# Two layers of attention and feed-forward: small VectorE steps moved to ScalarE and GpSimd, ternary weights taken later

## The chip, the cores and the metric

The kernel runs on one core of a Trainium2 chip. The metric is the device time of one execution in microseconds (us). The kernel before was timed in three runs: 1294.21, 1289.97 and 1292.45 us, median 1292.45. One more execution was profiled; times of single instructions come from it. PE is TensorE, DVE is VectorE, ACT is ScalarE, POOL is GpSimd, SP is the engine that issues most DMAs. "L842" is line 842 of the kernel before.

## What is computed

Two transformer layers over x of 2 batches, 1024 tokens, 256 features. In each, attention and feed-forward read the same normalised x and are both added to x.

```python
xn = layernorm(x)
x = x + attn0(xn) + ffn0(xn)     # attn0: 32 query heads of 8, 8 key heads, causal, rope, biases
xn = layernorm(x)
x = x + attn1(xn) + ffn1(xn)     # attn1: at each token, its 16 heads attend to each other
# ffn0: fp8 (e4m3) products: (gelu(x8 @ g0) * (x8 @ g1)) rounded to fp8, @ w_linear
# ffn1: silu(gate) * up, rms_norm, @ w_proj; both weights made ternary in groups of 64
```

## The kernel before, in words

**Layer 0** is one function, `attention0`. Its queries are cut into 16 tiles of 128 (batch 0 tiles 0 to 7, then batch 1 tiles 7 down to 0). A tile needs two passes over the scores. The first (`max_unit`) makes them on PE in pairs of PSUM banks from a pool of three (`ps_s`), and VectorE reduces each bank to row maxima (L842). `take_max` splits the maxima of a tile into three bf16 parts, `turn_max` transposes them on PE, copies them out of PSUM on VectorE (L867) and sends them through DRAM into the rows of `qlast`. The second pass (`weigh`) makes the scores again, transposed and with the maximum already subtracted by these rows, in banks of `ps_t` (four), and ScalarE takes the exponential (L906); `gather` multiplies by v (L914); `normalise` transposes and divides; `turn_rows` transposes again and copies out of PSUM on VectorE (L947); `output` multiplies by wo, and VectorE adds the product to x (L955).

PE's order is the program's order. The program is written in slots: one slot is a part of the second pass of the tile that is due, plus as many first-pass units of later tiles as a credit allows (`one_slot`, `advance`), at most three tiles ahead, plus one piece of the feed-forward. `after(n, f)` puts f some slots later. A tile's second pass begins ten slots after its maxima are complete (`LEAD`). The other engines take their instructions in an order that a scheduler chose when the program was built, each engine strictly in that order, so one that waits holds up all behind it.

**Feed-forward 0** (`ffn0`) runs in these slots, in 16 pieces of 256 hidden features (four token blocks, four pieces each). Per piece, ScalarE casts the gate and up products to bf16 (L284); VectorE does gelu's polynomial in five steps on 128x1024 bf16 (L287 to L291), ScalarE the tanh (L292), VectorE three more steps (L294 to L296), and `e4m3` rounds to fp8 (L180 to L185). With `check`, `e4m3` adds two steps that turn values beyond fp8's range into NaN (L188, L189). `weights0` rounds the six weight blocks in the same way at the start. `out_piece` makes the result of 128 tokens; ScalarE casts it to bf16 (L250), POOL adds it and a bias to x (L252, L253).

**Ternary weights** for layer 1 are made during layer 0, in 12 pieces (eight of w_gate_up, four of w_proj; `ternary`). Each is loaded from POOL's queue (L317); then one VectorE step (L320), a group sum on PE (L323), three VectorE steps (L325, L327, L328) and four POOL steps (L329 to L332), the last of which writes the bf16 result. The next piece's L320 overwrites a buffer that these POOL steps read. One piece is taken each time a tile's maxima are complete (`next_weights` in `advance`), so with the first twelve tiles. At the end `wgu_bf` is cast to fp32 (L1099), and `wp_bf` into the memory that K of batch 0 no longer needs (L1100).

**Projections** of layer 0 go from PSUM through VectorE (L722), POOL (L724) and a split into three bf16 parts by ScalarE and POOL (L699 to L703) to DRAM by DMAs from SP's queue (L753), and come back as `qmain` and `qlast`.

**Layer 1** (`layer1`) has an order written by hand with due times, mostly PE's work: f1gu (L605) and f1o (L636) are the feed-forward's products. The change doesn't touch it.

Of the kernel before, what the change touches and what calls it, by code (L numbers as in the profile page):

```python
# [10 lines left out]
F32 = mybir.dt.float32  # L11
BF = mybir.dt.bfloat16
# [7 lines left out]
P = 128  # L20
# [27 lines left out]
def two_layers(ctx: ExitStack, tc: tile.TileContext, a: dict, out: bass.AP):  # L48
# [73 lines left out]
        return w  # L122

    wgu_bf = cp.tile([P, 2, 2 * HID], BF, tag="wgu", name="wgu_bf")
    wp_bf = cp.tile([P, NHC, D], BF, tag="wp", name="wp_bf")


    k0 = [cp.tile([P, KV0 // 2, T], BF, tag=f"k0{n}", name=f"k0_{n}") for n in range(2)]
# [45 lines left out]
    def e4m3(dst, src, e, s, check):  # L174

        wide = src.dtype == F32
        as_int = I32 if wide else U16
        nc.vector.tensor_scalar(  # L180
            e.bitcast(as_int), src.bitcast(as_int), 0x7F800000 if wide else 0x7F80, None, ALU.bitwise_and
        )
        nc.vector.tensor_scalar(e, e, E4_MIN, 1.5 * 2.0**20, ALU.max, ALU.mult)
        nc.vector.tensor_tensor(s, src, e, ALU.add)
        nc.vector.tensor_tensor(dst, s, e, ALU.subtract)  # L185
        if check:
            y = e.bitcast(BF)[:, : dst.shape[1]]
            nc.vector.tensor_scalar(y, dst, E4_BIG, 0.0, ALU.mult, ALU.mult)  # L188
            nc.vector.tensor_tensor(dst, dst, y, ALU.add)  # L189


    added = [0] * NT
# [37 lines left out]
    def ffn0(pool, psp, weights):  # L230

        wg, wl = weights
        acts = {}

        def e_tile(dt, name):
            t = pool.tile([P, 1024], F32, tag="fe", name=name, bufs=1)
            return t if dt == F32 else t.bitcast(BF)[:, 0:1024]

        def out_piece(n, i):
            po = psp.tile([P, D], F32, tag="t", name=f"f0o{n}_{i}")  # L240
            for hc in range(NHC):
                nc.tensor.matmul(
                    po,
                    acts[n][hc // 2][:, hc % 2 * 512 + i * P : hc % 2 * 512 + (i + 1) * P],
                    wl[:, hc, :],
                    start=(hc == 0),
                    stop=(hc == NHC - 1),
                )
            ob = pool.tile([P, D], BF, tag="ob", name=f"ob{n}_{i}", bufs=1)
            nc.scalar.copy(ob, po)  # L250
            x_i = xs[4 * n + i]
            nc.gpsimd.tensor_tensor(x_i, x_i, ob, ALU.add)  # L252
            nc.gpsimd.tensor_tensor(x_i, x_i, bo_bc, ALU.add)  # L253
            add_done(4 * n + i)

        order = (0, 1, 3, 2)
        for m, n in enumerate(order):

            wide = pool.tile([P, 1024], F32, tag="fs", name=f"fsx{n}", bufs=1)
            xq = pool.tile([P, 2, 512], BF, tag="xq", name=f"xq{n}", bufs=1)  # L260
            e4m3(
                xq.rearrange("p k t -> p (k t)"),
                xnT[n].rearrange("p k t -> p (k t)"),
                e_tile(F32, f"fex{n}"),
                wide,
                False,
            )
            yield
            acts[n] = []
            for h2 in range(NHC // 2):  # L270
                nm = f"{n}_{h2}"
                wide = pool.tile([P, 1024], F32, tag="fs", name=f"fs{nm}", bufs=1)
                w1, f1 = (wide.bitcast(BF)[:, k * 1024 : (k + 1) * 1024] for k in range(2))
                g = pool.tile([P, 1024], BF, tag="fg", name=f"fg{nm}", bufs=1)
                w2 = pool.tile([P, 1024], BF, tag="fw", name=f"fw{nm}", bufs=1)
                for j in range(2):
                    hc = 2 * h2 + j
                    for u, to in enumerate((g, f1)):
                        ps = psp.tile([P, 512], F32, tag="t", name=f"gu{nm}_{j}{u}")
                        for k in range(2):  # L280
                            nc.tensor.matmul(  # L281
                                ps, wg[:, u, k, hc * P : (hc + 1) * P], xq[:, k, :], start=(k == 0), stop=(k == 1)
                            )
                        nc.scalar.copy(to[:, j * 512 : (j + 1) * 512], ps)  # L284
                    yield

                nc.vector.tensor_mul(w1, g, g)  # L287
                nc.vector.tensor_mul(w1, w1, g)
                nc.vector.tensor_scalar(w1, w1, GELU_C1, None, ALU.mult)
                nc.vector.tensor_add(w1, g, w1)  # L290
                nc.vector.tensor_scalar(w1, w1, GELU_C0, None, ALU.mult)  # L291
                nc.scalar.activation(w2, w1, AF.Tanh)  # L292
                yield
                nc.vector.tensor_scalar(w2, w2, 1.0, 0.5, ALU.add, ALU.mult)  # L294
                nc.vector.tensor_mul(w2, g, w2)
                nc.vector.tensor_mul(w2, w2, f1)  # L296
                yield
                act = pool.tile([P, 1024], BF, tag="act", name=f"act{nm}", bufs=5)
                e4m3(act, w2, e_tile(BF, f"fe{nm}"), wide, True)
                acts[n].append(act)  # L300
                yield
                if m and h2 == 0:
                    for i in range(4):
                        out_piece(order[m - 1], i)
                        yield
        for i in range(4):
            out_piece(order[-1], i)
            yield
# [23 lines left out]
        nc.gpsimd.tensor_tensor(dst, m, w, ALU.add)  # L332

    def ternary_units(pool, psp):
        for k in range(2):
            for c in range(4):
                cols = slice(c * 512, (c + 1) * 512)
                yield ternary(
                    pool, psp, wgu_bf[:, k, cols], a["w_gate_up"][k * P : (k + 1) * P, cols], f"g{k}{c}"
                )  # L340
        for c in range(4):
            yield ternary(
                pool,
                psp,
                wp_bf[:, 2 * c : 2 * c + 2, :].rearrange("p c d -> p (c d)"),
                a["w_proj"][c * 256 : (c + 1) * 256, :].rearrange("(c p) d -> p c d", p=P),
                f"p{c}",
            )
# [325 lines left out]
    def attention0(w, qlast):  # L674
# [11 lines left out]
        with ExitStack() as es:  # L686
# [176 lines left out]
            def turn_max(b, i, parts):  # L863
                ps = ps_t.tile([P, P], BF, tag="t", name=f"mt{b}{i}")
                nc.tensor.transpose(ps[: 3 * NH0], parts.rearrange("p a h -> p (a h)"), ident_bf)
                mt = pool.tile([3 * NH0, P], BF, tag="mt", name=f"mts{b}{i}", bufs=1)
                nc.vector.tensor_copy(mt, ps[: 3 * NH0])  # L867
                scr = dram.tile([3 * NH0, P], BF, tag="mscr", name=f"mscr{b}{i}")
                nc.sync.dma_start(out=scr, in_=mt)
                for e in range(2):  # L870
                    nc.sync.dma_start(
                        out=qst[b, i][1][HALF * e + AUG : HALF * e + AUG + 3],
                        in_=scr.rearrange("(a e n) t -> e a n t", a=3, e=2)[e],
                    )
# [66 lines left out]
            def turn_rows(b, i):  # L941
                rows = out_rows.pop((b, i))
                ps = ps_t.tile([P, 2, P], F32, tag="t", name=f"at{b}{i}")
                for k in range(2):
                    nc.tensor.transpose(ps[:, k, :], rows[:, k * P : (k + 1) * P], ident)
                oT = pool.tile([P, 2, P], F32, tag="oT", name=f"oT0_{b}{i}", bufs=1)
                nc.vector.tensor_copy(oT, ps)  # L947
                after(2, lambda: output(b, i, oT))

            def output(b, i, oT):  # L950
                po = ps_t.tile([P, D], F32, tag="t", name=f"ao{b}{i}")
                for k in range(2):
                    nc.tensor.matmul(po, oT[:, k, :], wo[:, k, :], start=(k == 0), stop=(k == 1))
                x_i = xs[8 * b + i]
                nc.vector.tensor_add(x_i, x_i, po)  # L955
                add_done(8 * b + i)


# [68 lines left out]
            def advance():  # L1027
                nonlocal at, credit, cost_left
                n, cost, unit = maxima[at]
                ready.extend(extra.pop(n, ()))  # L1030
                unit()
                if ready:
                    ready.pop(0)()
                at += 1
                credit -= cost
                cost_left -= cost
                if cost == 0:
                    done_at[n] = slot
                    next_weights()

            def one_slot(weights):

# [51 lines left out]
    with tc.tile_pool(name="w1", bufs=1) as wpool:  # L1094
        wgu = wpool.tile([P, 2, 2 * HID], F32, tag="wgu", name="wgu")
        for h in range(2):
            for g in range(2):
                cols = slice(g * HID + h * 512, g * HID + h * 512 + 512)
                nc.vector.tensor_copy(wgu[:, :, cols], wgu_bf[:, :, cols])  # L1099
        nc.vector.tensor_copy(wp, wp_bf)  # L1100
        layer1((wqk1, wv1), wgu, wp, *tables)


# [90 lines left out]
```

## Time and profile before

| | us |
|---|---|
| median of three runs | 1292.45 |
| the profiled execution | 1289.41 |
| its span, first to last instruction | 1287.2 |
| busy: PE, DVE, ACT, POOL | 1061.8, 794.4, 547.7, 244.5 |
| L842, the row maxima | 371.5 in 608 instructions |
| L906, the exponentials | 307.3 in 576 |

Outside the span lie 2.2 us of the execution. "Busy" of PE is modelled at its ends. "Granted clock" is the share of full speed that TensorE's clock was let run at, 0.895 on the mean.

Some instructions that the change removes or moves (mean us of one): L188 0.42, L189 0.68, L287 0.69 (median), L867 0.21, L947 0.42, L955 0.41, L1100 1.23; a ternary piece's L320 0.29, L325, L327, L328 0.68 each, and four POOL steps of 1.15. For comparison, ScalarE: L292 (tanh, 128x1024 bf16) 1.06, L250 (128x256 from PSUM) 0.37; POOL: L252 0.67, L253 0.73.

A row of the waits gives engine, line, what was waited for, then us in total, times, and the longest. A row of the timeline gives start, length, engine, line, operation, output and inputs, how many, and in brackets the idle time before and what ended it. "Start to start" of neighbouring VectorE instructions is some 0.07 us less than one's length.

### The profile page before, as it was taken

How to read it: one execution, taken by the hardware profiler on the slowest of the kernel's cores; microseconds unless marked ns; L12 is line 12 of the kernel's file. 1: busy time of each engine (PE TensorE's matmuls, PEld its weight loads, DVE VectorE, ACT ScalarE, POOL GpSimd, SP SyncE). 2: the span in 40 equal slices, each digit the busy share in tenths (PEclk: the TensorE clock that was granted, in tenths of full speed). 3: DMA queues.
4: the chain of work that ended last, by engine and by line, in shares of the span. 5: the costliest groups of instructions: out<-in, count | busy, mean ns of one | idle time of the engine just before them, and what ended most of it. 6: DMA issues, size and time to landing. Idle time of an engine off the chain costs nothing.

```text
span 1287.2 us, 19584 instructions
## 1 busy us (share of the span) xinstructions
PE 1061.8 (82%) x7484; PEld 504.0 (39%) x7484; DVE 794.4 (62%) x1494; ACT 547.7 (43%) x925; POOL 244.5 (19%) x239
## 2 busy tenths in 40 slices
PE   1475589779887798888798889998999999998884
PEld 0232233223232232223132333334566676675663
DVE  7988767986886889797868777516232332322220
ACT  1121243445364355655566655662242433424411
POOL 2433032111104002010111100104312222312200
PEclk9786688898899789998999989999899999998885
DMA  6321120110102001010100000006511331421202
GB/s 211 100 84 30 30 79 25 37 24 1 25 1 49 1 2 25 17 34 1 23 4 21 3 19 21 5 2 83 84 38 31 67 67 26 84 42 26 43 10 50
DMA packets 79782, 49.03 MB, mean 38 GB/s; under 512 B 32488, under 2 KB 74472, under 8 KB 79688
## 3 DMA queue, kind: packets, MB, share of 16 engines
q1 hardware_dynamic: 76584, 43.06, 15.4%
q0 software_dynamic: 3104, 4.72, 1.6%
q8 instruction: 59, 0.97, 0.3%
q14 instruction: 35, 0.29, 0.1%
HBM read 33.59 MB, written 15.73 MB: 38 GB/s over the span
## 4 chain that ended last, share of the span: by engine, by line
PE 54%; DVE 29%; POOL 7%; ACT 4%; issue 4%; DMA 2%; SPq 0%; POOLq 0%; ACTq 0%; DVEq 0%
DVE mx L842 13%; PE f1gu L605 9%; PE acc L914 7%; PE s L894 6%; PE f1o L636 5%; PE m L831 3%; PE sk L515 3%; PE sq L480 3%; PE m L813 2%; ACT p L523 2%; PE pqk L431 2%; PE s L813 1%; PE gu L281 1%; PE acc L530 1%; PE ao L581 1%
## 5 line engine op out<-in xcount | busy, mean ns | idle before, releaser
L842 DVE TENSOR_REDUCE mx<-m 128x1 f32<-128x512 f32 (+3 forms) x608 | 371.5, 654 | 89.9 <-PE m L813 58.6
L906 ACT ACTIVATE p<-s 128x512 f32<-128x512 f32 x576 | 307.3, 598 | 234.2 <-PE s L894 166.9
L914 PE MATMUL acc<-p,v 128*9 128x512 f32 x1152 | 172.1, 640 | 0.0
L831 PE MATMUL m<-k,qmain 64*128 64x512 bf16 (+3 forms) x384 | 101.6, 377 | 68.1 <-DVE mx L842 52.8
L605 PE MATMUL f1gu<-xnT,wgu 128*128 128x512 f32 x256 | 119.2, 610 | 0.0
L831 PE MATMUL m<-kmain,qmain 64*128 64x512 bf16 (+3 forms) x384 | 82.1, 333 | 36.3 <-DVE mx L842 34.9
L813 PEld LDWEIGHTS <-ident_h 64*128 64x128 bf16 x1088 | 60.2, 99 | 115.2 <-issue 81.5
L831 PEld LDWEIGHTS <-qmain 64*128 64x128 bf16 x768 | 49.1, 100 | 100.0 <-issue 60.1
L813 PE MATMUL m<-mask_q,ident_h 64*128 64x128 bf16 (+1 forms) x832 | 82.9, 243 | 3.6 <-DVE mx L842 3.2
L613 DVE TENSOR_TENSOR h<-f1gu,h 128x512 f32<-128x512 f32 x32 | 22.1, 691 | 102.3 <-PE f1gu L605 102.3
L894 PE MATMUL s<-qlast,k 35*128 35x512 bf16 x288 | 65.2, 406 | 10.4 <-DMA qlast<-mscr 10.4
L894 PE MATMUL s<-qmain,k 64*128 64x512 bf16 x288 | 68.2, 415 | 4.2 <-DVE att L937 2.3
L605 PEld LDWEIGHTS f1gu<-xnT,wgu 128*128 128x128 f32 x256 | 48.1, 197 | 49.8 <-issue 49.1
L617 POOL TENSOR_TENSOR sq<-h 128x512 f32<-128x512 f32 x28 | 29.1, 1039 | 190.8 <-DVE h L613 190.8
L894 PEld LDWEIGHTS <-k 64*128 64x128 bf16 (+1 forms) x576 | 23.4, 98 | 106.4 <-issue 99.0
L488 DVE TENSOR_REDUCE m<-sq 128x16 f32<-128x2048 f32 x16 | 36.7, 2291 | 43.8 <-PE sq L480 42.2
L894 PE MATMUL s<-qmain,kmain 64*128 64x512 bf16 x288 | 63.0, 397 | 0.8 <-ACT p L906 0.6
L636 PE MATMUL f1o<-k,h 128*128 128x256 f32 x256 | 61.7, 400 | 0.0
L894 PE MATMUL s<-qlast,klast 35*128 35x512 bf16 x288 | 61.1, 393 | 0.0
L636 PEld LDWEIGHTS f1o<-k,h 128*128 128x128 f32 x256 | 51.0, 201 | 9.3 <-issue 1.1
L252 POOL TENSOR_TENSOR x<-x,ob 128x256 f32<-128x256 f32 x16 | 10.7, 668 | 221.6 <-ACT ob L250 221.6
L169 PE MATMUL lnt<-ident,xn 128*128 128x128 f32 x64 | 15.5, 371 | 42.2 <-DVE xn L167 37.2
(264 smaller groups left out, 1593.5 us busy)
## 6 DMA issues: line engine op xcount, KB each, us to landing
qmain<-qscr SPq DMA_DIRECT2D x256, 32.0 KB
qkv<-all SPq DMA_DIRECT2D x16, 384.0 KB
qscr<-ptq SPq DMA_DIRECT2D x32, 96.0 KB
x<-in_x SPq DMA_DIRECT2D x16, 128.0 KB
spare_main<-in_w_gating POOLq DMA_DIRECT2D x4, 512.0 KB, 4.9
qs<-qkv SPq DMA_DIRECT2D x16, 128.0 KB
ks<-qkv SPq DMA_DIRECT2D x16, 128.0 KB
vs<-qkv SPq DMA_DIRECT2D x16, 128.0 KB
```

The costliest lines, as they stand in the source:

```text
L480: nc.tensor.matmul(ps[:, s, r, :], columns(q, slice(S * s, S * s + HD + 8), 4 * b + r), columns(k, slice(S * s, S * s + HD + 8), 4 * b + r ...
L488: nc.vector.tensor_reduce(m, ps, AX.X, ALU.max, negate=True)
L515: nc.tensor.matmul(ps[:, s, r, :], columns(k, slice(S * s, S * s + HD + 9), 4 * b + r), columns(q, slice(S * s, S * s + HD + 9), 4 * b + r ...
L605: nc.tensor.matmul(ps[g], wgu[:, k, g * HID + hc * P : g * HID + (hc + 1) * P], xnT[n][:, k, :], start=(k == 0), stop=(k == 1),)
L617: nc.gpsimd.tensor_tensor(sq, h, h, ALU.mult)
L636: nc.tensor.matmul(po, hs[hc // 2][:, hc % 2, i * P : (i + 1) * P], wp[:, hc, :], start=(hc == 0), stop=(hc == NHC - 1),)
L813: nc.tensor.matmul(out[e], ident_h[rows, t, :], rhs, start=start and t == 0, stop=stop and t == 1)
L831: nc.tensor.matmul(sc[e][:, s * width : (s + 1) * width], qst[b, i][0][rows, p, :], kst[b][0][rows, p // 4, lo : lo + width], start=not fo ...
L842: nc.vector.tensor_reduce(mx[b, i][:, part, e, pairs[0] : pairs[0] + n], sc[e][:, : n * width].rearrange("p (s k) -> p s k", s=n), AX.X, A ...
L894: nc.tensor.matmul(sc[e], kst[b][n][rows, u, j * P : (j + 1) * P], qst[b, i][n][rows, 4 * u : 4 * u + 4, :], start=n == 0, stop=n == 1 and ...
L906: nc.scalar.activation(p, sc[e], AF.Exp, scale=scale)
L914: nc.tensor.matmul(acc[32 * s : 32 * s + HD0 + 1, :], vst[b][:, j, 4 * G + s, :], ps[s], start=(j == 0), stop=(j == i),)
```

## The change

1. `e4m3` with `check`: L188 and L189 become one instruction that multiplies by a large number and by its inverse. A value out of range becomes infinite, no longer NaN.
2. `out_piece`: POOL adds ob, then multiplies ob by 0, and adds that too (an infinity becomes NaN there), before the bias: two more POOL instructions, 16 times.
3. gelu's first product, g times g (L287), is a Square on ScalarE.
4. The copies out of PSUM at L867 and L947 are made by ScalarE.
5. `output`: ScalarE copies wo's product into a buffer (shared with the attention rows "att"), POOL adds it to x; before, VectorE added it (L955).
6. Ternary pieces begin with the fourth tile, not the first, so the last comes with the fifteenth.
7. w_proj's ternary result is written in fp32 over K of batch 0 by the last POOL step; `wp_bf` and the cast L1100 are gone.

```diff
@@ e4m3
         if check:
-            y = e.bitcast(BF)[:, : dst.shape[1]]
-            nc.vector.tensor_scalar(y, dst, E4_BIG, 0.0, ALU.mult, ALU.mult)
-            nc.vector.tensor_tensor(dst, dst, y, ALU.add)
+            nc.vector.tensor_scalar(dst, dst, E4_BIG, 1.0 / E4_BIG, ALU.mult, ALU.mult)
@@ out_piece
+            nc.gpsimd.tensor_tensor(x_i, x_i, ob, ALU.add)
+            nc.gpsimd.tensor_scalar(ob, ob, 0.0, None, ALU.mult)
             nc.gpsimd.tensor_tensor(x_i, x_i, ob, ALU.add)
             nc.gpsimd.tensor_tensor(x_i, x_i, bo_bc, ALU.add)
@@ ffn0
-                nc.vector.tensor_mul(w1, g, g)
+                nc.scalar.activation(w1, g, AF.Square)
@@ ternary_units
-                wp_bf[:, 2 * c : 2 * c + 2, :].rearrange("p c d -> p (c d)"),
+                wp[:, 2 * c : 2 * c + 2, :].rearrange("p c d -> p (c d)"),
@@ turn_max
-                nc.vector.tensor_copy(mt, ps[: 3 * NH0])
+                nc.scalar.copy(mt, ps[: 3 * NH0])
@@ turn_rows
-                nc.vector.tensor_copy(oT, ps)
+                nc.scalar.copy(oT, ps)
@@ output
-                nc.vector.tensor_add(x_i, x_i, po)
+                wide = pool.tile([P, D], F32, tag="att", name=f"aos{b}{i}", bufs=1)
+                nc.scalar.copy(wide, po)
+                nc.gpsimd.tensor_tensor(x_i, x_i, wide, ALU.add)
                 add_done(8 * b + i)
@@ advance
                 if cost == 0:
                     done_at[n] = slot
-                    next_weights()
+                    if n >= 3:
+                        next_weights()
@@ two_layers
-    wp_bf = cp.tile([P, NHC, D], BF, tag="wp", name="wp_bf")
...
-        nc.vector.tensor_copy(wp, wp_bf)
```

## The prediction

> **What bounds the kernel now.** First the table of time by stretch, cut where the work changes: start, first maxima, both batches' attention, its end, layer 1. Columns: stretch, length, then busy time (instructions) of PE, PE's weight loads, DVE, ACT, POOL, granted clock, DMA share, GB/s.
>
> ```profile
> 0.00:74.00 74.00, 25.30 (x72) 11.72 (x72) 63.42 (x140) 9.35 (x16) 24.04 (x41) 0.84 0.50 148
> 74.00:147.00 73.00, 42.18 (x267) 20.91 (x268) 61.47 (x107) 13.53 (x21) 26.91 (x20) 0.69 0.17 44
> 147.00:838.00 691.00, 589.69 (x4325) 205.71 (x4325) 542.27 (x1033) 366.55 (x680) 98.36 (x98) 0.91 0.08 20
> 838.00:875.00 37.00, 34.70 (x226) 12.13 (x225) 7.28 (x23) 20.46 (x39) 1.35 (x1) 1.00 0.02 4
> 875.00:1287.20 412.20, 369.98 (x2599) 253.55 (x2597) 119.99 (x194) 137.85 (x170) 93.80 (x80) 0.91 0.29 51
> ```
>
> Up to 147 us VectorE is the bound (125 of 147 us busy). From 838 on it is TensorE, which the change hardly touches. Between, neither leads: PE 85%, DVE 78%. The waits of 0 to 804 us show it (us in total, times, longest):
>
> ```profile
> PE m L831 <- DVE mx L842: 87.7, 97, 4.2
> ...
> DVE mx L842 <- PE m L813: 53.5, 58, 3.6
> ...
> DVE tmg L320 <- POOL wgu_bf L332: 14.6, 4, 6.5
> ```
>
> PE waits for a maximum to free one of three score banks, and VectorE waits for the next scores, almost as long. So a microsecond taken off VectorE counts only where VectorE was the later one: the chain of waits says how often. Summing its pieces, DVE has 273 of 588 us between 147 and 740 (46%), 20 of 97 between 740 and 838, 1 of 37 after.
>
> **The start, to 147 us.** Before the first maximum (74.2) VectorE runs without a gap from 49 us on. The six weight conversions lose L189, 0.68 us each, about 0.65 from start to start; the new single instruction has the shape of L188 (0.42), which stays. 6 x 0.65 = 3.9. What it then waits for, the first scores, end at 67.4 in the trace of before, so the cover holds.
>
> Between 98 and 128 us, two ternary pieces go: each has L325, L327, L328 (0.6 start to start) and L320 (0.29), 2 x 2.1 = 4.2, and a wait of 1.04 for POOL, sum 5.2. One L189 (0.6) and one L867 (0.15) too. And this:
>
> ```profile
> 120.97 4.68 DVE L167 TENSOR_SCALAR xn<-x,mv,rs_yln 128x256 f32<-128x256 f32 x4
> 125.57 1.01 DVE L842 TENSOR_REDUCE mx<-m 128x1 f32<-128x384 f32 x2
> 126.50 0.72 DVE L167 TENSOR_SCALAR xn<-x,mv,rs_yln 128x256 f32<-128x256 f32 x2
> ```
>
> Four normalisations took 1.17 us each while POOL ran four ternary steps of 1.15 (120.7 to 125.5), and 0.36 each right after. The piece goes, so they shrink; PE's transposes pace them at about 0.5, so I take 4 x 0.6 = 2.4. Sum of the start: 3.9 + 5.2 + 0.75 + 2.4 = 12.3. I take 12, bounds 7 (the first maximum held by something else) and 16.
>
> One stall in the start stays. The rows, of PE, SP and ACT:
>
> ```profile
> 146.90 0.90 PE L894 MATMUL s<-qlast,k 35*128 35x512 bf16 x2 [10.39 <-DMA qlast<-mscr]
> ```
> ```profile
> 101.91 41.59 SPq L753 DMA_DIRECT2D qscr<-ptq  x5
> ```
> ```profile
> 136.18 1.06 ACT L292 ACTIVATE fw<-fs 128x1024 bf16<-128x1024 bf16 x1 [5.77 <-DVE fs L291]
> 137.14 0.60 ACT L699 CAST ptq<-q011y 128x512 bf16<-128x512 f32 x1
> ```
>
> SP stands 41 us in front of a store of q and holds back the transposed maxima behind it; q waits for ACT, where its cast L699 is queued behind the second tanh. POOL looks guilty (its ternary steps sit in its queue there), but it was ready at 126.4; ACT wasn't until 137.7. In the new order the cast is still behind that tanh, and behind one Square more. So I count nothing for this stall: it moves earlier with VectorE.
>
> **Attention, 147 to 838 us.** Removed VectorE work, by the time that the chain spends in each line here: L287 8.5 us, L189 2.5, L955 1.7, L947 1.3, L1100 1.2, L867 0.9. All of it, on the chain or not, is 14 x (0.69 + 0.68 + 0.21) + 13 x (0.42 + 0.41) + 1.2 = 34 us.
>
> Without L287 the chain loses 7.6. L287's 8.5 doesn't come whole, as its Square needs ACT:
>
> ```profile
> 766.41 0.59 ACT L284 CAST fg<-gu 128x512 bf16<-128x512 f32 x1
> 766.88 0.62 ACT L284 CAST fs<-gu 128x512 bf16<-128x512 f32 x1
> 767.04 0.69 DVE L287 TENSOR_TENSOR fs<-fg 128x1024 bf16<-128x1024 bf16 x1 [2.08 <-ACT fg L284]
> ```
>
> L287 starts as the gate's cast ends. The Square comes after the other cast (0.5 later) and costs what tanh costs at this shape (1.06), so L288 can start about 1.7 us after the gate's cast, not 0.7. In nine of the 16 pieces the new order puts two or more maxima (0.6 each) ahead of L288; in seven it has L288 at L287's place, and VectorE stands some 1.0 us more, with the maxima, and PE's scores behind them, queued behind it. 9/16 x 8.5 = 4.8; 7 x 1.0 x 46% = 3.2; left 1.6 (bounds -4 and 8.5).
>
> The ternary pieces: the third leaves 168 to 180 us, where PE stood 0.92 and 2.13 for maxima while L320 waited 6.5 for POOL: 3.0. Three come between 740 and 838: 3 x 2.3 us of VectorE and two or three waits of L320 of 2.3 (as the later pieces show), at the chain's share of 20/97: 12 x 0.2 = 2.5. Net 0.5. Their last POOL step writes fp32 over K of batch 0; the new order has it after that batch's scores, so its wait is long over. L332's row (1.15) may not hold for an fp32 result: nearest is 1.26 for fp32 sums of this size (L724), nothing for the end.
>
> ACT gets 14 x 1.06 + 14 x 0.3 (L867's copy, no row; between 0.2 and L250's 0.37) + 26 x 0.37 (L250's row for 128x256 out of PSUM) = 29 us more, 367 to 396 of 691. Behind them queue the exponentials; PE waits for these 3 us in all now and runs two slots ahead of them: 0 to 5, I take 0.5. The maxima's transposed copy is used ten slots later. POOL gets 16 x 3 x 0.67 = 32 us (L252's row[...]). POOL idles over 80% here, and x is read only by layer 1's statistics, L156, which waited four times for L253, 6.3 us together; four sums that take 1.4 longer bound that cost at 5.
>
> [...] The L167 rows agree (1.17 against 0.36), and the maxima, read from PSUM, show no such mark (0.6 under the same steps). If each of the 48 new POOL instructions stopped a VectorE instruction for half its 0.67, that is 16 us, at 46% 7 us off the gain. But it can only stop what is due: without the maxima (some 350 us here) VectorE is in such instructions under 190 of 691 us, 27%. 16 x 0.27 = 4.4, at 46% 2.0. I take 2.
>
> Sum: 7.6 + 1.6 + 0.5 - 0.5 - 2 = 7.2, say 7.5.
>
> **The end, 838 to 875, and layer 1.** PE is the bound, and the copies after the transposes cost on ACT (0.37) what they cost on VectorE (0.42). At the seam VectorE casts the gate weights from 873.83, right after L955; without it the casts start some 0.8 earlier, at PE's last product. POOL's memsets move behind four sums, and are needed much later. 1 us. Layer 1 has the same instructions: 0.
>
> **Sum.** 12 + 7.5 + 1 = 20.5 from the profiled execution's 1289.4 gives 1269; the three runs' median is 3 above that execution, one run within 0.6 of it. I say 1268.
>
> **The rivals.**
> - VectorE bounds the attention throughout: all 34 us go, and L287's place is filled with maxima: 12 + 34 + 1 = 47, 1242. For it: 35 of 40 us busy in some stretches (227 to 267). Against: its 88 us of waits for PE's scores there.
> - Only the start gains: [...] 12, 1277. For it: seven of 16 pieces have no cover.
> - POOL becomes what VectorE waits for, and it is slower. L320 of the next ternary piece waits for the four POOL steps of the one before, in POOL's one queue, which now holds x sums that wait for ACT and PE in turn. These waits are 2.3 to 4.7 us today. A block of sums (four of 0.67, 2.7) ahead of each, and its wait for ACT (about 1), makes each of eleven 3.7 longer: 41, less 20.5 is +20: 1310. It decides from 1.9 us more each. For it: 9.8 us of PE's stalls fall into such waits now. Against: in the new order most pieces' four steps stay together, and sums land between pieces.
> - That it changes nothing: VectorE's instructions fall from 1486 to 1399 in the built order, PE's order is the same but for the ternary products. Hardly possible.
>
> **Numbers.** Likeliest (1258 to 1276) 0.50, all of VectorE's time 0.22, only the start 0.17, near nothing 0.05, slower 0.06. Within 0.3% (3.9 us) is what a measurement here can't tell from no change. Faster 0.89, same 0.05, slower 0.06. Range 1238 to 1284: it takes in the full rival and the start alone, with their bounds.
>
> **What would show it.** First maximum near 70 us, L167 near 0.5 each, the 10 us stall of L894 still there but some 12 us earlier; L842's waits for scores longer, PE's for maxima shorter by about a tenth; new VectorE waits for the Square of about 1 us, seven or so; L320 waiting 2 to 5 us eleven times; layer 1's length unchanged. I am wrong if the stall before L894 goes (10 more), if L320's waits double, or if the granted clock of 147 to 838, 0.91, moves: a hundredth is about 6 us of PE's 590.

## The result and the profile after

The changed kernel takes 1286.01 us (median of five, 1285.05 to 1289.5), the kernel before 1292.3 us beside it: ratio 0.9962, 95% interval 0.9941 to 0.9984. Run again later it took 1287.66 us (six, 1284.84 to 1290.28), ratio 0.9954 (0.9938 to 0.997). So the change is worth some 5 to 6 us. 1268 us was predicted, some 20.5 below the profiled execution, with a range of 1238 to 1284; the time lies above it. The profiled execution took 1289.5 us (span 1287.7), the slowest of its five, at a mean clock of 0.886. The second profile of the same kernel took 1284.84 (span 1283.1), the fastest of its six, at 0.896; it is used beside the first, and as the fairer one beside the profile before, whose clock was 0.895.

The table of time by stretch, after the change (columns as before):

```profile
0.00:74.00 74.00, 24.02 (x72) 11.42 (x72) 62.62 (x134) 9.35 (x16) 27.02 (x42) 0.84 0.50 147
74.00:147.00 73.00, 46.77 (x312) 25.95 (x318) 53.25 (x100) 18.57 (x31) 11.41 (x9) 0.67 0.15 41
147.00:838.00 691.00, 596.09 (x4278) 204.86 (x4296) 519.97 (x971) 386.55 (x733) 142.96 (x153) 0.90 0.08 20
838.00:875.00 37.00, 33.02 (x203) 11.77 (x200) 3.37 (x12) 20.61 (x41) 1.65 (x3) 0.92 0.01 2
875.00:1287.70 412.70, 370.82 (x2600) 254.60 (x2600) 120.45 (x193) 137.81 (x170) 95.59 (x81) 0.91 0.29 51
```

The work moved as written: from 147 to 838 us VectorE is busy 22 us less, ScalarE 20 more, POOL 45 more. TensorE is busy 6 us more with no more products on record (4278, before 4325), and the clock of three stretches is lower, most of all from 838 on (1.00 to 0.92). The waits up to 804 us:

```profile
PE m L831 <- DVE mx L842: 79.1, 99, 3.8
...
DVE mx L842 <- PE m L813: 69.3, 62, 4.6
...
DVE tmg L319 <- POOL wgu_bf L331: 15.5, 6, 4.4
...
DVE fs L287 <- ACT fs L286: 9.2, 8, 3.8
...
DVE st L155 <- POOL x L252: 7.3, 5, 3.6
```

TensorE's wait for maxima fell by 8.6 us, and VectorE's for scores rose by 16: VectorE is later less often. The stall behind the transposed maxima stayed, as predicted, but it comes only 6.8 us earlier, not 12, and is 1.9 us longer:

```profile
140.15 0.76 PE L894 MATMUL s<-qlast,k 35*128 35x512 bf16 x2 [12.25 <-DMA qlast<-mscr]
```

To see where the time went, the traces are cut where a tile's maxima are complete (the first step of `take_max`), at the last copy of the weighted sums, and at layer 1's first product. Lengths in us, difference to before in brackets:

| stretch | before | after | after, 2nd profile | predicted |
|---|---|---|---|---|
| to the 3rd tile | 159.0 | 151.8 (-7.2) | 152.5 (-6.6) | -12 |
| 3rd to 4th | 50.3 | 43.4 (-6.9) | 42.1 (-8.2) | some -4 |
| 4th to 13th | 562.3 | 565.1 (+2.9) | 561.7 (-0.6) | some -6 |
| 13th to 16th | 65.8 | 74.1 (+8.2) | 74.0 (+8.1) | +2.5 |
| to the last copy | 30.8 | 31.7 (+0.9) | 31.7 (+0.9) | 0 |
| seam | 5.78 | 8.65 (+2.9) | 8.65 (+2.9) | -1 |
| layer 1 | 413.2 | 412.9 | 412.6 | 0 |

The last column splits the prediction's terms among these stretches. To the fourth tile some 14 of 16 us came; of the attention's gain behind it at most 0.6, and 12 us are lost after that. Layer 1, the same in all these kernels, takes 408.3 to 413.5 us in the profiles below, so one profile tells such differences only where rows show what lies behind them.

### The profile page after: what moved, and what is told of

Its sections match the earlier page's. It is cut to its first block, busy times and chain, and to the rows that moved or that the text cites. A ratio compares the mean times of both kernels' runs of the same rounds, so it can differ in the third digit from the quotient of the medians.

```text
span 1287.7 us, 19512 instructions
## 1 busy us (share of the span) xinstructions
PE 1070.7 (83%) x7458; PEld 508.6 (39%) x7484; DVE 759.6 (59%) x1407; ACT 572.9 (44%) x989; POOL 278.6 (22%) x287
## 3 DMA queue, kind: packets, MB, share of 16 engines
q1 hardware_dynamic: 76584, 43.06, 15.4%
## 4 chain that ended last, share of the span: by engine, by line
PE 52%; DVE 23%; POOL 7%; issue 6%; ACT 5%; DMA 4%; SPq 2%; POOLq 0%; ACTq 0%; DVEq 0%
DVE mx L842 11%; PE f1gu L605 8%; PE acc L914 7%; PE s L894 6%; PE f1o L636 5%; PE m L831 3%; PE sk L515 3%; PE sq L480 3%; PE m L813 2%; ACT p L523 2%; PE ao L581 1%; PE s L813 1%; PE acc L530 1%; PE gu L280 1%; SPq L766 1%
## 5 line engine op out<-in xcount | busy, mean ns | idle before, releaser
L914 PE MATMUL acc<-p,v 128*9 128x512 f32 x1152 | 175.9, 652 | 0.0
L831 PE MATMUL m<-kmain,qmain 64*128 64x512 bf16 (+3 forms) x384 | 85.3, 345 | 39.1 <-DVE mx L842 37.9
L957 POOL TENSOR_TENSOR x<-x,aos 128x256 f32<-128x256 f32 x16 | 11.8, 740 | 234.9 <-ACT aos L956 234.8
L894 PEld LDWEIGHTS <-kmain 64*128 64x128 bf16 x288 | 15.1, 94 | 83.1 <-issue 79.7
```

What stands on the lines that cost most here:

```text
L831: nc.tensor.matmul(sc[e][:, s * width : (s + 1) * width], qst[b, i][0][rows, p, :], kst[b][0][rows, p // 4, lo : lo + width], start=not fo ...
L894: nc.tensor.matmul(sc[e], kst[b][n][rows, u, j * P : (j + 1) * P], qst[b, i][n][rows, 4 * u : 4 * u + 4, :], start=n == 0, stop=n == 1 and ...
L914: nc.tensor.matmul(acc[32 * s : 32 * s + HD0 + 1, :], vst[b][:, j, 4 * G + s, :], ps[s], start=(j == 0), stop=(j == i),)
```

## The experiments

"The changed kernel" is the base unless said; the kernel before took 1291.5 to 1292.7 us beside each group.

**The memset in four pieces.** In the trace after, the first maximum still comes at 74.2, as before. The rows of VectorE, then of POOL:

```profile
68.73 3.82 DVE L186 TENSOR_SCALAR wl<-wl 128x1024 bf16<-128x1024 bf16 x1
```
```profile
68.76 3.50 POOL L735 MEMSET klast<- 128x4096 bf16 x1 [10.94 <-DVE wl L184]
```

L186, which takes 0.40 to 0.43 in its 21 other instructions, ends at 72.55, 0.29 after a memset that VectorE's own read (L184) sets free.

```diff
-   engine.memset(kst[b][1], 1.0)
+   if b: one memset for each kst[b][1][:, u], u = 0..3
```

> The changed kernel, with POOL's memset of the last K tile of batch 1 (3.5 us, one instruction) cut into four of 0.9 us. Theory: this memset [...] ate the start's gain (L186 took 3.82 us at 68.7, first maximum at 74.2 as before). Then the first maximum comes near 71.5 and the time falls by about 2.5, from 1286 to 1283.5. Rival: the first maximum waits for something else that lies under the memset, such as the second stage's statistics; then it stays at 74 and the time at 1286.

Measured: 1284.44 us (1282.04 to 1287.75). L186 takes 1.25 beside the four pieces, but the two normalisations behind it (L166) then take 1.76 instead of 0.73. The first maximum comes at 73.47, where some 71.5 was expected (74.22 and 75.33 in the changed kernel's two profiles), the third tile's maxima 2.0 us earlier. So the memset stood there; the 1.6 us by which the time is lower are within the spread.

**A buffer of its own for wo's copy.**

```diff
-   wide = pool.tile([P, D], F32, tag="att", ...)
+   wide = pool.tile([P, D], F32, tag="aos", ...)
```

> The changed kernel, with a buffer of its own for the copy of wo's product, which no longer shares the attention rows' one buffer. Theory: at the end of layer 0 the last rows (L937) wait for POOL's sum (1.2 us), PE for these rows (1.6) and then for ScalarE's copies; without the sharing the seam to layer 1 comes about 2 us earlier and the time falls from 1286 to 1284. Rival: the seam is later because the copy and the sum are a longer way to x than one VectorE instruction; then the seam and the time stay.

Measured: 1284.45 us (1281.14 to 1289.6). The stretch to the last copy falls from 31.7 to 30.8, as before the change, and the seam from 8.65 to 5.46: 4.1 us in the profile, while the median lies 1.6 and 3.2 below the changed kernel's two. Rows of the seam after the change, of VectorE, then of TensorE:

```profile
868.91 0.49 DVE L937 TENSOR_TENSOR att<-ot,z 128x128 f32<-128x128 f32 x2 [1.21 <-POOL x L957]
```
```profile
869.26 0.69 PE L945 MATMUL at<-ident,att 128*128 128x128 f32 x2 [1.63 <-DVE att L937]
869.75 1.91 PE L953 MATMUL ao<-wo,oT 128*128 128x256 f32 x4
872.17 2.08 PE L953 MATMUL ao<-wo,oT 128*128 128x256 f32 x4 [0.52 <-ACT oT L947]
874.77 3.78 PE L431 MATMUL pqk<-k,xnT 128*128 128x512 f32 x4 [0.52 <-ACT aos L956]
```

and with a buffer of its own:

```profile
865.73 0.53 PE L945 MATMUL at<-ident,att 128*128 128x128 f32 x2 [0.39 <-DVE att L937]
866.09 1.03 PE L953 MATMUL ao<-wo,oT 128*128 128x256 f32 x4
867.63 1.13 PE L953 MATMUL ao<-wo,oT 128*128 128x256 f32 x4 [0.52 <-ACT oT L947]
869.28 1.98 PE L431 MATMUL pqk<-k,xnT 128*128 128x512 f32 x4 [0.52 <-ACT aos L956]
```

The attention rows (L937) wait for POOL's sum, which reads the shared buffer, and TensorE's wait for them is 1.24 us longer (before the change it was 0.38). The same products take twice as long behind it (1.91 and 2.08 instead of 1.03 and 1.13): the clock reads 0.5 from 869.1 to 879.4 us.

**Which parts gain: ternary early, and late alone.** The first undoes parts 6 and 7, the second is the kernel before with part 6 alone.

```diff
@@ advance
-                    if n >= 3:
-                        next_weights()
+                    next_weights()
@@ ternary_units, two_layers: wp_bf and its cast are back
```
```diff
@@ the kernel before, advance
-                    next_weights()
+                    if n >= 3:
+                        next_weights()
```

> The changed kernel with parts 6 and 7 undone: ternary pieces from the first tile on, w_proj's pieces in their own bf16 buffer and cast at the end. Theory: taken late, the pieces win about 10 us before tile 3's maxima (195.3 against 209.3 us in all) and lose 7.5 between 760 and 822; undone, tile 3's maxima come near 205, the stretch from the maxima of the thirteenth tile to those of the fifteenth takes 52 us as before, not 59.6, and the time is about 1288. Rival: the end's loss is not theirs but the x sums' on POOL; then the start is lost and nothing comes back: 1294.

> The kernel before with part 6 alone: ternary pieces from the fourth tile on, nothing else changed. Theory: about 10 us won by tile 3's maxima, 7.5 lost between 760 and 822, so 1292.3 becomes 1290. Rival (the prediction's own sum for this part): 5.2 + 2.4 + 0.5 won and nothing more, 1284.

Measured: ternary early 1292.73 us (1286.27 to 1298.43; ratio 1.000, 0.9981 to 1.0019); late alone 1285.19 (1278.42 to 1287.61). So part 6 alone gives as much as the whole change, and parts 1 to 5 together nothing, though VectorE is busy 30.5 us less with them (763.9, before 794.4). Parts 4 and 7 were not tried alone. My theory at this point was that TensorE waits only for the maxima themselves, so that small steps on VectorE are free.

**That theory against the prediction's: two kinds of VectorE work left out.** The first leaves out seven of gelu's eight steps, the second a quarter of each full bank's maxima.

```diff
-                nc.vector.tensor_mul(w1, w1, g)
...
-                nc.vector.tensor_mul(w2, w2, f1)
```
```diff
-                        sc[e][:, : n * width].rearrange("p (s k) -> p s k", s=n),
+                        (the same)[:, :, : width * 3 // 4 if n * width == 512 else width],
```

> The changed kernel without seven of the eight VectorE steps of gelu (L287 to L290 and L293 to L295; the tanh reads the Square, and its result goes to the rounding as it is). So part of the computation is left out. By the rows of the changed kernel this takes 16 x (0.74 + 0.52 + 0.72 + 0.49 + 0.46 + 0.69 + 0.81) = 71 us of busy time off VectorE, and 9 us of waits for the Square. Theory now held: TensorE waits for VectorE only while a maximum itself is being made (three score banks), and small steps fill the time in which VectorE would otherwise wait for scores; so less than a fifth comes back, 5 to 14 us: 1272 to 1281. Rival (the prediction's way of counting): VectorE is late in 46% of this time, so 46% of 71 comes back, 33 us: 1253.

> The changed kernel with the maxima taken over only three quarters of each full 512-wide score bank (384 of 512 columns, or 3/4 of each of the 2 or 4 parts); the rest of each bank's scores is made but not looked at, so part of the computation is left out. By the rows (0.682 at 512 columns, 0.551 at 384) 480 x 0.13 = 63 us leave VectorE, about as many as in the kernel without gelu's steps, but each from an instruction that frees a score bank. Theory: TensorE's waits for maxima (81 us in the changed kernel) shrink with each maximum; 40 to 60% of the 63 come back, 25 to 38 us: 1248 to 1261. Rival (VectorE's total load counts, whichever instruction it is in): the same as for gelu's steps left out, within 5 us.

Measured: 1248.58 us (1246.72 to 1253.13) without gelu's steps, 1258.29 (1256.5 to 1260.53) with short maxima. My theory falls: small steps are worth no less than maxima. For 60.0 and 60.9 us that VectorE is busy less (71 and 63 by the lengths of the rows), 37 and 28 come back. Half of that is TensorE's idle time, the other half its busy time: against the second profile, 16.8 and 19.4 us without gelu's steps, 14.7 and 13.1 with short maxima. The rows from the 4th to the 13th tile's maxima, of before, after and without gelu's steps:

```profile
209.31:771.57 562.26, 474.20 (x3392) 156.94 (x3390) 452.69 (x841) 298.41 (x554) 80.18 (x79) 0.91 0.07 17
```
```profile
195.26:760.40 565.14, 483.96 (x3370) 159.66 (x3394) 431.85 (x787) 316.03 (x597) 107.43 (x116) 0.89 0.07 17
```
```profile
187.98:721.26 533.28, 465.65 (x3395) 155.86 (x3394) 386.34 (x701) 316.21 (x598) 108.25 (x116) 0.94 0.08 19
```

Length less TensorE's busy time is its idle time: 88.1, 81.2, 67.6. So the change took 6.9 us off it (7.8 in the second profile), about what was predicted. But the busy time rose by 9.8 (7.2) for the same products, at a clock of 0.89 (0.90) instead of 0.91; without gelu's steps it fell by 8.5, at 0.94. Busy time multiplied by clock, taken in steps of 1 us, is 431.1 before, 429.7 after (433.0 in the second profile) and 434.6 without gelu's steps: the work is the same within some 1%, its speed isn't. So the clock makes up all of the 9.8, and 5.3 of the 7.2.

**The clock.** It reads 1.0 or 0.5 and nothing else, and in each of the 18 traces every change lies on one grid of 3.413 us. The time lost to half clock from the 4th to the 13th tile, counted as slice times (1 less clock), idle moments included, is 51.2 us before, 61.7 after (54.6 in the second profile), 34.1 without gelu's steps. Each window of the grid, from 147 to 875 us in all 18 traces, set beside the clock of the next:

| clock in the window | TensorE busy in it | windows | next one at half clock |
|---|---|---|---|
| full | under 50% | 261 | 259 |
| full | 50 to 60% | 129 | 79 |
| full | 60% and more | 2774 | 18 |
| half | under 70% | 95 | 95 |
| half | 70 to 90% | 181 | 166 |
| half | 90 to 99% | 96 | 57 |
| half | 99% and more | 305 | 4 |

So in these traces half clock followed 259 of the 261 full-clock windows that were less than half busy, and full clock came back after 301 of the 305 half-clock windows that were busy 99% and more. (Busy time is modelled at its ends. In layer 1 the split is less clean: in the traces of before and after, full-clock windows busy 60% and more are followed by half clock 11 times of 185 there.) The longest half-clock stretch after the change, as windows, with the rows ahead of it on VectorE and on TensorE:

```profile
370.00:398.00 28.00, 24.91 (x157) 8.81 (x152) 18.48 (x35) 16.13 (x32) 8.66 (x8) 1.00 0.08 19
398.00:430.00 32.00, 25.24 (x88) 5.60 (x88) 27.21 (x45) 9.28 (x17) 4.32 (x4) 0.52 0.15 34
```
```profile
396.94 1.42 DVE L287 TENSOR_TENSOR fs<-fs,fg 128x1024 bf16<-128x1024 bf16 x1 [1.94 <-ACT fs L286]
398.28 1.27 DVE L842 TENSOR_REDUCE mx<-m 128x1 f32<-128x512 f32 x2
399.48 1.40 DVE L288 TENSOR_SCALAR fs<-fs 128x1024 bf16<-128x1024 bf16 x1
```
```profile
399.01 0.58 PE L831 MATMUL m<-k,qmain 64*128 64x512 bf16 x1 [1.96 <-DVE mx L842]
```

VectorE waits 1.94 us for the new Square with a maximum queued behind L287, then L287 and L288 take 1.42 and 1.40 beside POOL's ternary steps (0.74 and 0.52 on the mean). TensorE stands 1.96 and is busy 35% of the window from 394.7; from 398.1 the clock reads 0.5, for 30.7 us. VectorE has hardly an idle moment there (27.2 of 32): each window holds another wait, so that TensorE is busy 54 to 92% of it, and the one of 100% is the last at half clock. The kernel before has such a stretch too, from 412 to 440 us with a break of 3.4, behind a stall of 4.2 us; it lost 11.9 us, this one 15.4.

How much of this is the change's, and how much chance, is open. From the 4th to the 13th tile TensorE was busy at half clock for 86.6 us before, for 109.2 and 97.4 after, and for 96.8 to 102.3 in the kernels with parts 1 and 2, part 5 or part 6 alone; there is only one profile of the kernel before. Over all executions the mean clock is 0.892 before (109 of them) and 0.891 after (11). Within the kernel before it goes from 0.887 to 0.902, and each 0.01 less goes with 6.7 us more (correlation -0.85).

**Three ternary pieces earlier.** Extra pieces with tiles 4, 5 and 6, w_proj's in bf16 as before.

```diff
                     if n >= 3:
                         next_weights()
+                    if n in (4, 5, 6):
+                        after(8, next_weights)
```

> The changed kernel with the ternary pieces starting at the fourth tile as there, but three extra ones with tiles 4, 5 and 6 (slots 8 later), so that none falls into the last tiles; w_proj's pieces keep their bf16 buffer and the cast at the end (1.2 us of VectorE beside the seam), since K of batch 0 is in use then. Theory: the changed kernel is 11 us ahead at the 13th tile and 3 us at the 16th because three pieces fall into 760 to 835 us, where VectorE has no idle time; taken earlier they cost less than the 7.5 us lost there: the 16th tile's maxima are 7 to 11 us ahead of the kernel before, and the time is 1279 to 1283. Rival: a piece costs the same 2.5 us wherever it is taken in the attention, so the lead is lost earlier: 1286, the 16th tile 3 us ahead.

Measured: 1290.9 us (1283.07 to 1297.54). Refuted: the last tiles do keep their time (66.8 us, 65.8 before), but from the 4th to the 13th tile it takes 572.1 us, 7 more than the changed kernel, idle 88.4 (81.2). Three pieces cost some 7 us in either place, and the time is above what both theories said.

**gelu's first product on VectorE.**

```diff
-                nc.scalar.activation(w1, g, AF.Square)
+                nc.vector.tensor_mul(w1, g, g)
```

> The changed kernel with gelu's first product back on VectorE (part 3 undone): 16 x 0.69 = 11 us more VectorE, and no waits for the Square (9.2 us in the changed kernel, 8 times). Theory: what VectorE gains by the step it loses in waiting for ScalarE: within 2 us of the changed kernel, 1284 to 1288. Rival (prediction): the step's net is 1.6 us in the chain's time, so undoing it gives 1287.6; the other rival, that VectorE's load counts in full: 1297.

Measured: 1285.66 us (1282.05 to 1287.3, 22 executions). Part 3 gains nothing that shows.

**Mends together, the moves undone, the sum undone, and no NaN.** Diffs: the small set has the four-piece memset, the buffer of its own and the line above. "No moves" has the memset and `tensor_mul(w1, g, g)`, both `nc.scalar.copy(mt | oT, ps)` as `nc.vector.tensor_copy`, and the sum on VectorE. The third has only the sum on VectorE:

```diff
-                wide = pool.tile([P, D], F32, tag="att", ...)
-                nc.scalar.copy(wide, po)
-                nc.gpsimd.tensor_tensor(x_i, x_i, wide, ALU.add)
+                nc.vector.tensor_add(x_i, x_i, po)
```

and the fourth:

```diff
-            nc.gpsimd.tensor_tensor(x_i, x_i, ob, ALU.add)
-            nc.gpsimd.tensor_scalar(ob, ob, 0.0, None, ALU.mult)
```

> The changed kernel with three mends together: klast's memset of batch 1 in four pieces, a buffer of its own for wo's copy, and gelu's first product back on VectorE. Theory: each mend alone gave 1.5, 1.5 and 0.3 us; the first frees the start, the second the seam, so they add: 1281 to 1284. At the seam, from ScalarE's last copy of the weighted sums to layer 1's first product, 5.5 us (8.7 in the changed kernel, with 5 us of half clock; 4.4 to 5.8 without). Rival: what is won before 875 us is taken back by the clock, and only chance separated these runs: 1286.

> The changed kernel with parts 3, 4 and 5 undone (gelu's first product, both copies out of PSUM and wo's sum are VectorE's again) and the memset in four pieces: left of the change are the shorter rounding with its two POOL steps, the later ternary pieces and w_proj's place. Theory: the moved steps take TensorE's waits down by 4 to 8 us in the attention, and the clock, the last tiles and the seam take that back: within 2 us of the kernel with the memset in four pieces (1284.4), so 1282 to 1287, with TensorE idle near 88 us from the fourth to the thirteenth maximum (81 in the changed kernel). Rival (the prediction's sum): the moved steps are worth 6 us, so 1290.

> The changed kernel with wo's sum back on VectorE (part 5 undone), straight out of PSUM: no copy on ScalarE, no shared buffer, no sum on POOL. Theory: the seam loses its wait for the shared buffer (1.63 us) and the half clock behind it (5 us at half rate), 3 us; the last tiles lose POOL's sums in front of the ternary steps, 1; VectorE gets 16 x 0.41 = 6.6 back, 3 at 46%: 1284 to 1287. Rival: moving the sum is a gain as the prediction counted it (1.7 of the chain, and 1 at the seam): 1288 to 1290.

> The changed kernel without the two added POOL steps of part 2 (x + ob, ob times 0; the sum of ob stays), so part of the computation is left out: a value out of fp8's range stays infinite. 32 POOL instructions, 0.66 and 0.85 us, 24 us of POOL, leave. Theory: [...] its waits for the ternary steps (21.7 us in the changed kernel, 14.6 before) fall back: 2 to 4 us, 1282 to 1284. Rival: POOL has room, nothing waits: 1285 to 1287.

Measured:

| kernel | us, median (range) | ratio, 95% interval | seam |
|---|---|---|---|
| small set | 1278.28 (1275.88 to 1280.17) | 0.9894 (0.9872 to 0.9915) | 5.46 |
| no moves | 1278.55 (1275.82 to 1287.07) | 0.9911 (0.9877 to 0.9944) | 5.78 |
| sum on VectorE | 1278.74 (1277.02 to 1280.28) | 0.9899 (0.9878 to 0.9919) | 5.45 |
| no NaN | 1280.45 (1276.35 to 1285.23) | 0.9911 (0.9883 to 0.9938) | 8.65 |

All four are some 6 to 9 us faster than the changed kernel, more than either theory said. Undoing parts 3, 4 and 5, with the memset cut, is no loss but a gain; undoing part 5 alone is as good. The two POOL steps of part 2 cost more than the 2 to 4 expected. The mean clock over the executions is higher in all four: 0.900, 0.899, 0.898 and 0.896, beside 0.891. At 6.7 us per 0.01 that would be 6, 6, 5 and 4 us, an estimate.

**Is it part 5?** The changed kernel again beside three others: the kernel before with part 5 alone, the kernel before with parts 1 and 2 alone (diffs as in the change), and the changed kernel with the sum on VectorE and the memset in four pieces.

> The changed kernel once more, unaltered, so that it stands on the same chip and beside the same runs of the kernel before as the three here. If part 5 is what takes the gain, 1285 to 1288, and 6 to 8 us above the kernel with wo's sum on VectorE. If the distance to that kernel was the chip's or chance, 1279 to 1282.

> The kernel before with part 5 alone: ScalarE copies wo's product into a buffer shared with the attention rows, POOL adds it to x. Theory: the seam costs 3.2 us (8.65 us from the last copy to the first product, where it was 5.78, with 5 us of half clock), sums in POOL's queue cost some 2 to 4 more in the attention, 6.6 us of VectorE's time give 3 back: 1293 to 1297 beside 1292. Rival (the prediction): 1.7 of the chain and 1 at the seam are gained: 1289.

> The kernel before with parts 1 and 2 alone: the shorter rounding, and the two POOL steps that make NaN of an infinity. Theory: VectorE loses 22 steps of 0.68 us (15 us; 4 of them in the start, where the 3.5 us memset holds it up instead), worth 5 in the attention at 46%; the 32 POOL steps cost up to 5 again (the changed kernel without them took 5.6 less): 1289 to 1292. Rival (the prediction): 4.65 in the start and 2.3 in the attention[...]: 1286.5.

> The changed kernel with part 5 undone and klast's memset in four pieces. Theory: 7.3 us for part 5 and 1.5 for the memset add up: 1276 to 1279, the best of all. Rival: what these mends free is given back by the clock, as with the earlier ones: 1279 to 1281, no better than part 5 undone alone.

Measured: the changed kernel 1287.66 us; part 5 alone 1291.01 (1288.04 to 1294.96), ratio 0.9987 (0.9976 to 0.9999); parts 1 and 2 alone 1290.06 (1282.27 to 1293.49), ratio 0.9982 (0.9969 to 0.9995); the last 1278.74 (1275.76 to 1280.04), ratio 0.9877 (0.986 to 0.9895), with the lowest ratio of all that compute everything, but no lower median than the sum on VectorE alone; whether these two mends add up isn't told.

So the distance of 7 to 9 us is real, but part 5 alone on the kernel before doesn't cost it; my expectation of 1293 to 1297 failed. Its seam says why in part:

```profile
875.94 0.52 PE L945 MATMUL at<-ident,att 128*128 128x128 f32 x2 [1.64 <-DVE att L937]
876.30 1.03 PE L953 MATMUL ao<-wo,oT 128*128 128x256 f32 x4
877.84 1.13 PE L953 MATMUL ao<-wo,oT 128*128 128x256 f32 x4 [0.52 <-DVE oT L947]
879.49 1.98 PE L431 MATMUL pqk<-k,xnT 128*128 128x512 f32 x4 [0.52 <-ACT aos L956]
```

The same wait of 1.64 us, with no half clock behind it: its seam is 6.70 us, not 8.65. The windows of the clock's grid around the stall, in the changed kernel:

```profile
865.72:869.13 3.41, 1.18 (x9) 0.70 (x7) 0.73 (x4) 1.23 (x3) 0.72 (x1) 1.00 0.00 0
869.13:872.55 3.42, 2.77 (x7) 1.86 (x8) 0.28 (x2) 0.65 (x2) 0.07 (x1) 0.50 0.00 0
```

and with part 5 alone:

```profile
871.68:875.09 3.41, 1.89 (x12) 1.06 (x10) 0.90 (x3) 0.96 (x2) 0.26 (x1) 1.00 0.00 0
875.09:878.50 3.41, 2.04 (x9) 1.48 (x10) 0.91 (x3) 0.37 (x1) 1.11 (x2) 1.00 0.00 0
```

There the stall lies in one window, busy 1.18 of 3.41 us (35%), and the next is at 0.50; here it is split between two, busy 55 and 60%, both at 1.00.

## Why the prediction was wrong, step by step

In the second profile 4.1 of the 20.5 us came. Of the 16.4 missing, some 1 is lost to the fourth tile, 5.4 from there to the 13th, 5.6 in the last tiles and 4.8 behind them, and layer 1 gives 0.6 back.

**The start: one term wrong.** To the third tile 7.2 and 6.6 us were gained, 12 predicted; to the fourth 14.1 and 14.8, some 16 predicted. Late ternary alone is 6.6 us ahead at the third tile and 11.1 at the fourth, where the sum had 7.6 and 10.6 for the two pieces, L167 and the third piece. The weights' shorter rounding and the two small steps (3.9 + 0.75) failed in the step "What it then waits for, the first scores, end at 67.4 in the trace of before, so the cover holds": what came due first was POOL's memset, 3.5 us, which the same rounding releases.

**Attention, "Sum: 7.6 + 1.6 + 0.5 - 0.5 - 2 = 7.2".** This sum holds for TensorE's idle time (-6.9; -7.8 in the second profile). The step that failed is the one that takes less waiting for as much less time: TensorE's busy time, taken as fixed, rose by 9.8 and 7.2, of which the clock is 9.8 and 5.3. The prediction named the clock among the signs that it is wrong and had no term for it. That a change of this kind lowers the clock isn't shown: on the mean of all executions it did not fall. The price of 46% was in part luck: two large cuts gave 62% and 46% of VectorE's time back (52% and 44% by the rows' lengths), but in idle time, which is what the chain counts, only 28% and 24%; the clock made up the rest.

**The Square** waits eight times, 9.2 us together, about as predicted, and part 3 nets nothing; that the longest stretch of half clock begins behind such a wait wasn't in the sum. With the Square undone there is still such a stretch, 409 to 433 us, so the Square isn't its only cause.

**The late pieces, "12 x 0.2 = 2.5".** The rows from the 13th to the 16th tile, before, with late ternary alone, and after:

```profile
771.57:837.42 65.85, 61.69 (x601) 25.89 (x593) 45.68 (x110) 41.99 (x80) 5.59 (x8) 1.00 0.05 13
765.78:836.92 71.14, 63.42 (x604) 26.55 (x596) 53.16 (x122) 42.09 (x80) 22.17 (x21) 0.98 0.06 14
760.40:834.45 74.05, 65.82 (x604) 27.14 (x596) 51.24 (x115) 43.88 (x85) 27.66 (x30) 0.96 0.06 13
```

Late ternary alone loses 5.3 us: idle time rises from 4.2 to 7.7, and the clock falls from 1.00 to 0.98. The chain's share of 20/97 was that of a stretch without these pieces; with them VectorE is later more often. In the changed kernel it is 8.2 us, 4.1 of them idle time and 4.1 busy time, at a clock of 0.96. One such place, on VectorE, ScalarE and TensorE:

```profile
804.15 0.29 DVE L319 TENSOR_SCALAR tmp<-twp 128x512 uint16<-128x512 uint16 x1 [2.57 <-POOL k L331]
```
```profile
804.77 0.20 ACT L140 ACTIVATE rs_sln<-rs_vln 128x4 f32<-128x4 f32 x1 [1.97 <-DVE rs_vln L139]
```
```profile
805.38 0.27 PE L831 MATMUL m<-kmain,qmain 64*128 64x256 bf16 x1 [1.90 <-DVE mx L842]
```

L319 waits for POOL with a statistic and the maxima queued behind it; ScalarE, its table just changed for that statistic (1.28 us, from 801.52), waits 1.97 in turn, and TensorE stands 1.90.

**The end, "1 us" gained: lost 2.9.** That the copy shares a buffer with the attention rows stands in the list of the change; the prediction put no price on it. The last tile's rows can't be written until POOL has added the tile before (a wait of 1.21 us), and at half clock the products behind took 1.91, 2.08 and 3.78 us instead of 1.03, 1.13 and 1.98. With a buffer of its own the stretch to the last copy and the seam take 0.3 us less than before the change, not 1.

**POOL as the slower rival** did not come. The waits for the ternary steps went from 24.1 us (8 waits) to 21.7 (9) over the whole run, not up by eleven times 3.7. (The expectation for the kernel with no NaN sets 21.7 beside 14.6, but the 14.6 are only a part of those before.) But POOL's added steps do cost: without part 2's two the kernel is 5.6 to 7.2 us faster. In the traces some 3 of these are idle time of TensorE (77.6 against 80.3 and 81.2); the higher mean clock, 0.896, would make 4 by the estimate above. The 2 us that the prediction took off for VectorE steps beside POOL's were my estimate; what the rows after the change show of this is L287 and L288 at 1.42 and 1.40 beside the ternary steps, and the maxima of 512 columns at 0.68 on the median, both where POOL was busy throughout (41 of them) and where it was idle (367).

**Part 5's 7 to 9 us** are located to 5.6, by the second profile against that of the sum on VectorE: the seam 3.2, the last tiles 1.6 (74.0 against 72.4 us), the stretch up to the last copy 0.9. The two profiles differ by 6.5 us in all. Over the executions the clock is 0.898 instead of 0.891, some 5 us by the estimate, part of which is the half clock at the seam. Why the clock is higher there, and why part 5 costs this only beside the other parts, stays open.

Right were the stall that stayed, TensorE's waits for maxima, shorter by a tenth, ScalarE's costs (Square 1.08, copies 0.27 to 0.39) and layer 1.

## What to carry to other kernels

Where one engine waits for another, the chain's share is a first price of a saved step, but check what the freed engine will meet next: a memset, a shared buffer or a queue that was late without harm before. The 1.6 us stall of TensorE at the seam cost 0.9 us in one kernel and 2.9, with half clock behind it, in another, so judge a change by idle time and by busy time at the granted clock separately, over several executions. Steps moved from VectorE to POOL were not free here, where the attention rows waited 1.21 us for POOL's sum, which read a buffer they share: the kernel with wo's sum left on VectorE (1278.74 us), and the one with the sum on POOL, a buffer of its own and two more mends (1278.28), were faster than the change as it was made.

## What the hardware showed that was not expected

- The same 1.6 us stall at the seam cost 0.9 us in one kernel, where the clock stayed at 1.00, and 2.9 in another, where it then read 0.5 for 10.2 us. In the first it was split between two windows of 3.413 us (busy 55 and 60%), in the second it lay in one (35%). Over the 18 traces, from 147 to 875 us, full-clock windows busy under 50% were followed by half clock 259 times of 261, those busy 60% or more 18 times of 2774.
- Half clock lasted at a load at which full clock did too: after a window at half clock that was 70 to 90% busy, the next was at half clock 166 times of 181, while from full clock windows of that kind were followed by half clock 4 times of 673.
- With VectorE work left out TensorE's mean clock over the executions was higher: 0.910 without gelu's steps and 0.901 with short maxima (six each), 0.892 before. At 6.7 us per 0.01 the first would be some 12 of the 43 us to the kernel before; an estimate.
- Beside a POOL memset (3.50 us, 128x4096 bf16) a VectorE instruction of one input, in place (L186, 128x1024 bf16), took 3.82 us instead of 0.41. Beside the memset in four pieces (4.06 together) it took 1.25.
